# ScalarE zeroes the stacks, and TensorE transposes the identity between the foldings of the set-up

## The chip, the core and the metric

The kernel runs on one core of a Trainium2 chip. A core has a matrix engine (TensorE, PE in the profile, with its weight loads as PEld), a vector engine (VectorE, DVE), a scalar engine (ScalarE, ACT), a general engine (GpSimd, POOL) and an engine that here only issues transfers (SyncE, SP). The metric is the time of one execution on the device in microseconds; the lower, the better.

## What is computed

The reference applies two attention layers to x, which has 32 sequences of 256 tokens with 256 features. What matters of it here:

```python
# layer 0: linear attention, 8 heads of 32
xn = _ln(x, ln_w, ln_b)
q = softmax((xn @ Wq + bq).reshape(b, t, h, dh), axis=-1)
k = softmax((xn @ Wk + bk + (1.0 - src_mask) * -1000000.0).reshape(b, t, h, dh), axis=1)
v = ((xn @ Wv + bv) * src_mask).reshape(b, t, h, dh)
att = einsum('bnhd,bnhl->bhdl', k, v)
y = einsum('bnhd,bhdl->bnhl', q, att).reshape(b, t, d)
scale, shift = split(silu(emb) @ W_emb + b_emb)
x = x + silu(_ln(y, ln2_w, ln2_b) * (1 + scale) + shift) @ W_out + b_out
...
# layer 1: softmax attention, 16 heads of 16, then the same output block
att = softmax(einsum('bnhl,bmhl->bnmh', q, k) + (1.0 - mask) * -1000000.0, axis=2)
y = einsum('bnmh,bmhl->bnhl', att, v)
```

The weight and the bias of each first layer norm are constants of the inputs, so the kernel multiplies them into Wq, Wk and Wv once, before it uses these. This is the folding. A wide product is done as three products of float32r parts: each operand is split into a high part and the rest (a low part).

## The kernel before, in words

The program consists of one set-up (`prepared`) and of 32 sequences (`sequence(b)`), each with four parts a to d: layer 0 up to its values (a), the output block of layer 0 (b), the scores of layer 1 (c) and its output (d). Each step is an `Op` with an engine and a time. The times stand in two tables written out in the file: `SET_UP` for the set-up, and `STARTS` for a sequence, to which 26.2851 times the number of the sequence is added. `in_order` sorts all steps by these times and emits them; an engine executes its instructions in exactly that order. So a step that waits holds up everything that comes later on its engine. A list in `SET_UP` has one time for each use of a step's name, in the order in which the program creates them.

The set-up steps that matter here:

- `identity` (lines 264 to 267, GpSimd) makes the 128x128 identity `ident`. `identity_r` (269 to 275, VectorE) copies it to float32r and sums it to `fold` and `fold4`.
- `warmed` (277 to 280, TensorE) transposes the identity 16 times into a PSUM bank that nobody reads.
- `qk_zeros` (507 to 510, GpSimd) zeroes a stack: a pair of tiles, `qs` and `ks`, of 128 partitions by 2048 float32r each. There are three stacks (`ROOM["qk"]`), so there are six memsets. The times -674.55, -379.66 and -61.21 place two stacks at the head of GpSimd's queue and one after its first step of sequence 0. `qk_made` (512 to 515, SP) then writes a constant row into a stack.
- `w_high` (304) on ScalarE and `w_low` (307) on VectorE split a weight into its two parts (`parts`). The first of them is `wout0`: its `w_high` stands at -439.51, its `w_low` at -307.80.
- `w_rep` (316 to 323), `bias_scaled` (331) on VectorE, and `w_sums` (342 to 351) on TensorE, `w_scaled` (353) on VectorE are the folding of one weight. Per folding TensorE does two 6x256 matmuls (line 345) and four 128x256 matmuls in float32 (line 349). On VectorE the order is: `identity_r`, `token_terms`, the second `w_rep`, `w_low` of `wout0`, the first `w_rep`, `bias_scaled`. The first folding needs the last two.
- On TensorE the order is: `warmed`, `terms_turn` (449), the foldings of w02, w00 and w01, `e_product` (388), the turn of sequence 0 (565), the folding of w12, `e_sums` (399), the turn of sequence 1, and then the first products (558).
- In ScalarE's order, `split_high` of sequence 0 (752, at 4.18) comes directly before `k_kept` of sequence 1 (818, at -19.92 + 26.2851 = 6.37). `attention` (889, in the profile under 888) needs `k_kept`, and `k_sums` (895) and `blocks` (901) on VectorE need `attention`.

Of the kernel before, what the change touches and what calls it, by code (L numbers as in the profile page):

```python
# [10 lines left out]
F32 = mybir.dt.float32  # L11
# [5 lines left out]
P = 128  # L17
# [6 lines left out]
    bank=8, xt=9, nrm=4, x=4, h=2, g=6, k0=3, ek=1, mk=1, q0=1, y=2, eqT=2, v0=2, att=1, qkp=1, qk=3,  # L24
# [43 lines left out]
    identity_r=(-702.04,), load_bias=(-276.37,), load_bout=(-13.79, 53.66), load_cols=(-670.58,),  # L68
    load_cond=(-544.29,), load_emb=(-258.80, -217.52, -180.67, -207.44, -42.77, -14.95, -48.76, -2.89),
    load_masks=(-359.47,), load_w=(-291.77, -528.39, -390.22, -548.16, -39.72, -33.64, -88.51, -232.84),  # L70
    mask_terms=(-103.15,), p_made=(91.90, 5.63), qk_made=(-52.44, 60.07, 77.11), qk_zeros=(-61.21, -379.66,
    -674.55), qkp_made=(30.64,), terms0_store=(-141.84,), terms_rows=(-172.06,), terms_store=(-42.73,),
    terms_turn=(-333.70,), token_terms=(-574.41,), v0_made=(-369.51, -279.71), va_made=(-36.90, 52.97),
    w_high=(-50.10, -64.76, -198.98, -439.51, 25.73, 18.32, 14.13, -231.47), w_low=(-39.74, -58.97, -95.39,
    -307.80, 29.41, 24.14, 30.22, 4.56), w_rep=(-292.96, -366.10), w_scaled=(-76.66, -94.61, -210.46, 20.45,
    9.77, -47.81), w_sums=(-179.39, -114.53, -238.08, 19.55, 7.28, -54.52), warmed=(-409.56,),
    zero_one=(-762.96,), zero_one_store=(-98.07,),
)
LATE = dict(D=dict(late=2.2))
# [85 lines left out]
def tile_two_layers(ctx: ExitStack, tc: tile.TileContext, a: dict, out: bass.AP):  # L165
# [11 lines left out]
    nc = tc.nc  # L177
    x = a["x"]
    B, S, D = x.shape
# [7 lines left out]
    NSLOT = NU * NC  # L187
# [4 lines left out]
    const = ctx.enter_context(tc.tile_pool(name="const", bufs=1))  # L192
# [5 lines left out]
    def bank(dtype=F32):  # L198
        return psum.tile([P, 512], dtype, tag="bank", name="bank", bufs=ROOM["bank"])

    def f(ap):
        return ap.bitcast(F32)
# [5 lines left out]
    ident = const.tile([P, P], F32, name="ident")  # L208
    ident_r = const.tile([P, P], F32R, name="ident_r")
    fold = const.tile([P, B], F32, name="fold")  # L210
    one = const.tile([P, 1], F32, name="one")
    minus_half = const.tile([P, NBLOCK], F32, name="minus_half")
    fold4 = const.tile([P, P], F32, name="fold4")
    cols = const.tile([P, NCOL + 2 * NTOK], F32, name="cols")
# [26 lines left out]
    done = {}  # L241
# [11 lines left out]
    def prepared():  # L253
# [3 lines left out]
        def op(engine, time, run, *after, take=(), give=(), **more):  # L257
            ops.append(Op(engine, time, run, after, take, give, **(LATE.get(engine, {}) | more)))
            return ops[-1]
# [4 lines left out]
        def identity():  # L264
            make_identity(nc, ident)
            nc.gpsimd.memset(one, 1.0)
            nc.gpsimd.memset(minus_half, -0.5)

        def identity_r():
# [11 lines left out]

        o_cols = op("D", 0.3, load_cols)
        o = op("G", 0.9, identity)
        op("P", 0.11 * NWARM, warmed, o, take=("bank",), give=("bank",))
        done["ident"] = op("V", 0.13, identity_r, o)


# [152 lines left out]
        o = op("D", 0.3, load_bias)  # L440
# [17 lines left out]
        o = op("V", 0.2, token_terms, o_cols)  # L458
        o = op("P", 0.5, terms_turn, o, done["ident"], take=("bank",))
        o = op("V", 0.35, terms_rows, o, give=("bank",))  # L460
# [15 lines left out]
        o = op("D", 0.3, load_cond)  # L476
        o = op("A", 0.2, cond_tanh, o)
# [20 lines left out]
        o = op("D", 0.3, load_masks)  # L498
        o = op("V", 0.6, mask_terms, o)
# [7 lines left out]
        def qk_zeros():  # L507
            s.qk.append(qk_all.pop(0))
            for buf in s.qk[-1]:
                nc.gpsimd.memset(f(buf), 0.0)  # L510

        def qk_made():
            qk_bufs.append(s.qk.pop(0))
# [14 lines left out]
        o = op("G", 0.6, zero_one)  # L528
        o_stored = op("D", 0.3, zero_one_store, o)
        o_z = o_stored  # L530
        for n in range(ROOM["qk"]):
            o = op("G", 4.0, qk_zeros)
            o_z = op("D", 0.8, qk_made, o, o_z, give=("qk",))

        o_rep = norm_rows(1, o_cols)
# [630 lines left out]

    ctx.enter_context(tc.manual_schedule(engines=None))
    return in_order(prepared, [lambda b=b: sequence(b) for b in range(B)], ROOM)


# [67 lines left out]
```

## Time and profile before

| | |
|---|---|
| median of 3 runs | 918.5 us (918.21 to 922.14) |
| the profiled execution, own time | 914.85 us |
| its span | 912.7 us |
| TensorE busy | 864.9 us (95%) |
| VectorE busy | 813.5 us (89%) |
| ScalarE busy | 700.2 us (77%) |
| GpSimd busy | 692.4 us (76%) |
| mean granted clock of TensorE | 0.97 |

The span runs from the first to the last instruction on the core; the execution's own time is 2.15 us longer. A line of the timeline gives the start and the duration in microseconds, the engine, the line of the program, the instruction, what it writes from what, its shape, and in brackets how long the engine had been idle and what ended the wait. A line of the windows gives, for one stretch of time, the busy microseconds of each engine, the number of its instructions, and the TensorE clock granted (1.00 is full).

### The profile page before, as it was taken

The numbers are of one execution on the slowest core, as the hardware profiler recorded it, in microseconds if no ns is written. First come the engines' busy times: TensorE is split into PE (matmuls) and PEld (weight loads), VectorE is DVE, ScalarE is ACT, GpSimd is POOL, SyncE is SP. The second block draws the span as 40 slices with busy tenths as digits, with TensorE's granted clock in tenths as the row PEclk, the third lists the DMA queues.
The fourth block names the chain that finished last, engine by engine and source line by source line (L and its number), as shares of the span: only waits on it lengthen the run. The fifth ranks groups of instructions, "written<-read, shape, count | busy, mean of one in ns | idle before, by whom it ended". The sixth has DMA issues, their size and how long they took to land.

```text
span 912.7 us, 25210 instructions
## 1 busy us (share of the span) xinstructions
PE 864.9 (95%) x9494; PEld 705.0 (77%) x9494; DVE 813.5 (89%) x2235; ACT 700.2 (77%) x1420; POOL 692.4 (76%) x893
## 2 busy tenths in 40 slices
PE   6878899999999999999999999999999999999973
PEld 3667787888888888888888888888888888877642
DVE  6797989999999999999999999999999999999843
ACT  1365588788888898888888888888888888877762
POOL 5254567888888888988888888988888877775441
PEclk6799999999999999999999999999999999999985
DMA  6302222322232222223222212332233221222200
GB/s 215 108 16 88 84 81 81 102 104 97 103 103 74 89 71 90 102 104 103 96 104 86 86 60 92 104 102 104 96 104 103 71 82 57 87 86 86 95 14 24
DMA packets 56767, 81.09 MB, mean 89 GB/s; under 512 B 5407, under 2 KB 30021, under 8 KB 56646
## 3 DMA queue, kind: packets, MB, share of 16 engines
q1 hardware_dynamic: 56646, 79.47, 25.4%
q8 instruction: 76, 1.25, 0.6%
q14 instruction: 45, 0.37, 0.1%
HBM read 19.52 MB, written 8.55 MB: 31 GB/s over the span
## 4 chain that ended last, share of the span: by engine, by line
PE 79%; DVE 15%; POOL 2%; issue 1%; ACT 1%; DMA 0%; POOLq 0%; DVEq 0%; ACTq 0%
PE bank L558 37%; PE bank L1122 12%; PE bank L1100 9%; PE bank L1033 8%; PE bank L565 5%; DVE mx L1044 5%; PE bank L916 3%; PE bank L814 1%; PE bank L888 1%; DVE st L591 1%; PE bank L650 1%; PE bank L349 1%; DVE th L746 1%; DVE ident_r L270 1%; DVE yb L1138 1%
## 5 line engine op out<-in xcount | busy, mean ns | idle before, releaser
L1044 DVE TENSOR_REDUCE mx<-bank 128x2 f32<-128x512 f32 x512 | 324.9, 673 | 15.0 <-PE bank L1033 14.7
L1113 ACT ACTIVATE p<-bank 128x512 f32<-128x512 f32 x512 | 270.2, 600 | 84.1 <-PE bank L1100 78.5
L558 PE MATMUL bank<-xh,w_hi 128*128 128x256 f32 x512 | 153.1, 299 | 0.1
L558 PE MATMUL bank<-xl,w_hi 128*128 128x256 f32 x512 | 144.3, 282 | 1.2 <-DVE xl L707 1.2
L558 PE MATMUL bank<-xh,w_lo 128*128 128x256 f32 x512 | 143.9, 281 | 0.0
L1122 PE MATMUL bank<-p,va 128*32 128x256 f32 x2048 | 140.0, 386 | 0.1
L558 PE MATMUL bank<-wout_hi,hp 128*128 128x256 f32 x512 | 112.9, 302 | 10.0 <-ACT hp L752 9.5
L982 POOL TENSOR_TENSOR qk_lo<-nrm,qk_hi 128x512 fp32r<-128x512 f32 x58 | 74.7, 1287 | 56.5 <-ACT nrm L978 56.5
L1100 PE MATMUL bank<-qs,ks 64*128 64x256 f32 x1024 | 109.0, 311 | 4.3 <-DMA qs<-m_row 3.1
L1033 PE MATMUL bank<-ks,qs 64*128 64x256 f32 x1024 | 105.4, 307 | 1.0 <-DVE mx L1044 0.3
L1100 PEld LDWEIGHTS bank<-qs,ks 64*128 64x128 f32 x1024 | 73.8, 187 | 37.0 <-ACT p L1113 22.6
L558 PEld LDWEIGHTS bank<-xh,w_hi 128*128 128x128 f32 x512 | 97.1, 190 | 5.1 <-DVE mx L1044 0.4
L558 PEld LDWEIGHTS bank<-xl,w_hi 128*128 128x128 f32 x512 | 97.3, 190 | 1.6 <-DVE xl L707 1.6
L558 PEld LDWEIGHTS bank<-wout_hi,hp 128*128 128x128 f32 x512 | 86.3, 196 | 15.6 <-ACT hp L752 10.1
L1033 PEld LDWEIGHTS bank<-ks,qs 64*128 64x128 f32 x1024 | 73.6, 185 | 31.3 <-issue 13.4
L558 PEld LDWEIGHTS bank<-xh,w_lo 128*128 128x128 f32 x512 | 96.9, 189 | 0.0
L613 POOL TENSOR_SCALAR nrm<-xt,mv,off 128x256 f32<-128x256 f32 x116 | 65.0, 571 | 29.0 <-DVE off L608 26.1
L1122 PEld LDWEIGHTS bank<-p,va 128*32 128x32 f32 x2048 | 55.0, 109 | 41.1 <-ACT p L1113 1.8
L728 POOL TENSOR_TENSOR xt<-xt,bout 128x512 f32<-128x512 f32 x64 | 82.5, 1288 | 3.1 <-DMA bout<-in_bout_dram 3.1
L756 POOL TENSOR_TENSOR hp<-th,hp 128x512 fp32r<-128x512 f32 x58 | 74.9, 1292 | 9.1 <-ACT hp L752 9.1
L558 PE MATMUL bank<-w_hi,xh 128*128 128x256 f32 x256 | 78.2, 305 | 0.0
L707 POOL TENSOR_TENSOR xl<-nrm,xh 128x512 fp32r<-128x512 f32 x58 | 73.6, 1288 | 4.3 <-ACT nrm L703 4.3
(138 smaller groups left out, 2153.9 us busy)
## 6 DMA issues: line engine op xcount, KB each, us to landing
ks<-qk_hi SPq DMA_DIRECT2D x64, 256.0 KB
qs<-qk_hi SPq DMA_DIRECT2D x64, 256.0 KB
xt<-in_x_dram SPq DMA_DIRECT2D x32, 256.0 KB
ks<-qk_lo SPq DMA_DIRECT2D x32, 256.0 KB
qs<-qk_lo SPq DMA_DIRECT2D x32, 256.0 KB
out_dram<-xt SPq DMA_DIRECT2D x32, 256.0 KB
mk<-t_dram SPq DMA_DIRECT2D x32, 128.0 KB
raw<-in_w_dram SPq DMA_DIRECT2D x8, 256.0 KB
```

What stands on the lines that cost most here:

```text
L558: nc.tensor.matmul(o, left, right, start=(n == 0), stop=(n == len(pairs) - 1))
L565: nc.tensor.transpose(ps[:, ds(c * S + t * P, P)], src[:, t, ts(c, P)], ident)
L613: (nc.vector if s.quick else nc.gpsimd).tensor_scalar(s.nrm[:, t, :], get()[:, t, :], s.mv[:, t, 1:2], s.off[:, t : t + 1], ALU.mult, ALU.add)
L707: engine.tensor_tensor(s.xp[1], s.whole, f(s.xp[0]), ALU.subtract)
L728: nc.gpsimd.tensor_tensor(s.x, s.x, bout[:, i : i + 1, :].to_broadcast([P, NT, D]), ALU.add)
L756: engine.tensor_tensor(s.hp[1], s.th, f(s.hp[0]), ALU.subtract)
L982: engine.tensor_tensor(s.qkp[1][:, :, c], s.qk_ps[c], f(s.qkp[0][:, :, c]), ALU.subtract)
L1033: nc.tensor.matmul(ps[w][:, ts(m, S)], s.qs[half(w), u, c, ts(m, P)], s.ks[half(w), u, c, :], start=True, stop=True,)
L1044: nc.vector.tensor_reduce(s.mx[:, :, w, u, c], halves(s.s_ps[0, c, u][w]), AX.X, ALU.max, negate=True)
L1100: nc.tensor.matmul(ps[w][:, ts(m, S)], s.ks[half(w), u, c, ts(m, P)], s.qs[half(w), u, c, :], start=True, stop=True,)
L1113: nc.scalar.activation(s.pt[c, u][:, w], s.s_ps[1, c, u][w], AF.Exp)
L1122: nc.tensor.matmul(s.yT_ps[c][32 * j : 32 * j + 32, ts(v, S)], s.va[:, m, 8 * c + 4 * v + j, :], s.pt[c, 2 * v + j // 2][:, j % 2, ts(m, S ...
```

## The change

The six zeroing instructions leave GpSimd and become copies on ScalarE, whose source is a column of zeros (`nothing`) read 2048 times. The times of `qk_zeros` in the table change too: two stacks now stand at the head of ScalarE's queue (-650.21 and -640.66), and the third at 5.55, between `split_high` of sequence 0 and `k_kept` of sequence 1. TensorE gets four steps `heated`, each of six transposes of the identity into a bank that nobody reads. Their times put one after each of the foldings of w02, w00 and w01, and one after `e_product`. GpSimd gets one more small memset.

```diff
-    ... qk_zeros=(-61.21, -379.66, -674.55), ...
+    ... qk_zeros=(-650.21, -640.66, 5.55), ...
-    ... warmed=(-409.56,),
+    ... warmed=(-409.56,), heated=(-209.0, -146.0, -105.0, -80.0),
...
+    nothing = const.tile([P, 1], F32, name="nothing")
...
             nc.gpsimd.memset(one, 1.0)
+            nc.gpsimd.memset(nothing, 0.0)
             nc.gpsimd.memset(minus_half, -0.5)
...
         o = op("G", 0.9, identity)
+        done["zero"] = o
         op("P", 0.11 * NWARM, warmed, o, take=("bank",), give=("bank",))
+
+        def heated():
+            ps = bank()
+            for n in range(6):
+                nc.tensor.transpose(ps[:, ts(n % 4, P)], ident, ident)
+
+        for n in range(4):
+            op("P", 0.66, heated, o, take=("bank",), give=("bank",))
...
         def qk_zeros():
             s.qk.append(qk_all.pop(0))
             for buf in s.qk[-1]:
-                nc.gpsimd.memset(f(buf), 0.0)
+                nc.scalar.copy(buf.rearrange("p u c n -> p (u c n)"), nothing.to_broadcast([P, NSLOT * S]))
...
         for n in range(ROOM["qk"]):
-            o = op("G", 4.0, qk_zeros)
+            o = op("A", 4.0, qk_zeros, done["zero"])
             o_z = op("D", 0.8, qk_made, o, o_z, give=("qk",))
```

More of the change, by code (lines that the diff above doesn't have):

```diff
@@ L70 @@
     load_masks=(-359.47,), load_w=(-291.77, -528.39, -390.22, -548.16, -39.72, -33.64, -88.51, -232.84),
-    mask_terms=(-103.15,), p_made=(91.90, 5.63), qk_made=(-52.44, 60.07, 77.11), qk_zeros=(-61.21, -379.66,
-    -674.55), qkp_made=(30.64,), terms0_store=(-141.84,), terms_rows=(-172.06,), terms_store=(-42.73,),
+    mask_terms=(-103.15,), p_made=(91.90, 5.63), qk_made=(-52.44, 60.07, 77.11), qk_zeros=(-650.21, -640.66,
+    5.55), qkp_made=(30.64,), terms0_store=(-141.84,), terms_rows=(-172.06,), terms_store=(-42.73,),
     terms_turn=(-333.70,), token_terms=(-574.41,), v0_made=(-369.51, -279.71), va_made=(-36.90, 52.97),
@@ L75 @@
     -307.80, 29.41, 24.14, 30.22, 4.56), w_rep=(-292.96, -366.10), w_scaled=(-76.66, -94.61, -210.46, 20.45,
-    9.77, -47.81), w_sums=(-179.39, -114.53, -238.08, 19.55, 7.28, -54.52), warmed=(-409.56,),
+    9.77, -47.81), w_sums=(-179.39, -114.53, -238.08, 19.55, 7.28, -54.52), warmed=(-409.56,), heated=(-209.0, -146.0, -105.0, -80.0),
     zero_one=(-762.96,), zero_one_store=(-98.07,),
```

## The prediction

> **What bounds the kernel now.** I read the page first, then the windows of the fill and the drain, then the chain of waits and the timeline of the first 100 us.
>
> ```profile
> PEclk6799999999999999999999999999999999999985
> ...
> PE 79%; DVE 15%; POOL 2%; issue 1%; ACT 1%; DMA 0%; POOLq 0%; DVEq 0%; ACTq 0%
> ```
>
> From 100 us to 855 us TensorE has work almost all the time and makes up the chain. The change touches nothing there: it can only move the moment at which that stretch begins. So all is decided in the set-up, and a microsecond won or lost on its chain is one at the end, as the order of every engine is fixed. The first slices show a low clock, and the timeline shows why the set-up begins late:
>
> ```profile
> 1.80 1.82 POOL L510 MEMSET qs<- 128x2048 f32 x1
> 1.81 7.11 DVE L270 CAST ident_r<-ident 128x128 fp32r<-128x128 f32 x1 [0.29 <-POOL ident masks.py:199]
> ...
> 3.90 0.63 ACT L305 ACTIVATE wout_hi<-raw 128x512 fp32r<-128x512 f32 x1 [1.91 <-DMA raw<-in_w_dram]
> ...
> 7.02 1.82 POOL L510 MEMSET ks<- 128x2048 f32 x1
> ...
> 10.10 0.68 DVE L308 SCALAR_TENSOR_TENSOR wout_lo<-raw,wout_hi 128x512 fp32r<-128x512 f32 x1
> ...
> 11.70 1.21 PE L345 MATMUL bank<-bias,ident 6*128 6x256 f32 x2 [1.51 <-DVE bias L332]
> ```
>
> VectorE's small cast lasts 7.11 us, exactly as long as GpSimd's four memsets (1.80 to 8.84); a cast of half its partitions takes 0.24 us at 17.88. The memsets hold VectorE up. Behind the cast stand `wout_lo`, the first `w_rep`, the bias, and so TensorE's first folding at 11.70.
>
> The windows, each 3.41 us, show busy TensorE without clock:
>
> ```profile
> 1.55:4.97 3.42, 3.14 (x15) 3.14 (x16) 3.16 (x2) 1.27 (x3) 3.42 (x5) 1.00 0.82 209
> 4.97:8.38 3.41, 0.33 (x3) 0.09 (x1) 3.41 (x2) 0.00 (x0) 3.41 (x3) 1.00 0.84 301
> 11.79:15.21 3.42, 3.42 (x7) 1.94 (x8) 0.26 (x1) 0.63 (x1) 0.00 (x0) 0.50 0.82 267
> ...
> 28.86:32.27 3.41, 3.41 (x18) 3.41 (x18) 1.59 (x5) 1.27 (x2) 0.89 (x2) 0.50 0.48 126
> 32.27:35.68 3.41, 3.01 (x25) 2.81 (x24) 2.95 (x6) 0.00 (x0) 0.00 (x0) 1.00 0.76 225
> ```
>
> After the window, the first column is busy TensorE and the third from the end its clock. I chose these limits since the clock changes at 8.38, 32.25, 861.7, 865.1, 875.3, 882.1 and 892.4, and all distances are multiples of 3.41 us. From 11.7 to 32.25 the foldings run at half clock.
>
> **Part 1: two stacks at the head of ScalarE's queue.** GpSimd's four memsets go, and VectorE's cast ends at about 2.1 instead of 8.92. But VectorE executes in order, and its `wout_lo` needs ScalarE's `wout_hi`, which now stands behind four copies of 128x2048. No row shows such a copy. ScalarE's 128x128 activation takes 0.293 us, its 128x512 one 0.630, so 0.878 ns per element; its 128x512 casts in a row start 0.52 us apart. Estimate: 0.52 + 1536 x 0.878 ns = 1.87 us each, 7.5 us for four, hence from 1.9 to about 9.4. Then the table load (1.28 us in its row). It carries the line of `wout_hi`, the first ACTIVATE; the profile names copies COPY or CAST, so I take it to follow the four copies. Then `wout_hi` ends at 1.90 + 7.48 + 0.1 + 1.28 + 0.63 = 11.39, `wout_lo` begins at 11.43, and the folding, 1.60 us after it as before (10.10 to 11.70), at 13.03: **1.33 us later**. If the load still comes first, 11.74: 0.04 later. So the stall that goes is replaced by a wait for ScalarE. Nothing else gains: GpSimd's next work is at 17.58, and `cond_tanh` (4.44 before) is used at 16.08. SP's next weight load waits for `wout_lo` and slips with it; the last of the first four embedding weights is issued at 13.13 and used at 21.15.
>
> The page "ScalarE: Activation LUTs", section "What ACT_TABLE_LOAD costs", gives 186 ns + 0.833 ns per element, about 1.89 us for such a copy, and adds a drain of 1.38 us to the load. By that drain the folding would begin at 14.4; the trace has a load of 1.28 us and no such drain in view.
>
> **Part 2: the transposes.** In the trace 16 of them from 1.83 on start 0.213 us apart and last 421 ns; the last ones last 313 and 272, and 272 is what one lasts at full clock at 109 us. So transposes raise the clock: a window 92% full did it, and the idle one after it took it away at 8.38.
>
> The page "TensorE: Matmul & The Clock Gate", section "Part 4: PE-mode transpose", says that full clock doesn't engage for transposes. It speaks against this change: by it `heated` is pure cost, +5.1 us as in rival B. The durations above contradict it.
>
> Whether six are enough is open. Half clock: folding 3.15 us (11.70 to 14.85), `e_product` 1.87, turn 1.05, six transposes 6 x 0.213 = 1.28. Full clock: folding 0.62 + 1.07 = 1.69 (57.93 and 58.55), `e_product` 0.98 (43.92), turn 0.53, transposes 0.66 (four last 0.60 with their tail). Up to the end of sequence 0's turn: before 24.14 - 11.70 = 12.44; with the four groups 12.44 + 5.12 = 17.56 at half, 3 x 1.69 + 0.98 + 0.53 + 4 x 0.66 = 9.22 at full. If the clock comes g after the first folding's begin, 9.22 + 0.475 g, thus -3.2 + 0.475 g. After the turn, full clock brings VectorE's `eq` (32.45, 8.31 after the turn) forward to where VectorE's and ScalarE's own work puts it: activations 1.9, then a low part 0.7, `nrm` 0.8, `xl` 0.6, statistics 1.0, scaling 0.8, low part 0.7 = 6.5, so 1.8 sooner. In sum **-5.0 + 0.475 g**.
>
> A folding has 2.0 us of full-array matmuls and 1.15 us with six rows, which I count as nearly idle. Windows with up to about 62% such work kept half clock (892.4 to 895.9: ten matmuls of 0.213 us); those with about 84% or more raised it (878.7 to 882.1). A folding with a group lasts 4.43 us; a window of 3.41 us in it is filled 59% to 87%, depending on where it falls. With 70% as the point, about half of the positions rise in the first window (g about 4.6), a third in the second (9.3), the rest at 13.5. I take g = 6.8, **-1.8 us**; the ends are -3.4 (g = 3.4) and +5.1.
>
> **Part 3: the third stack at 51.8.**
>
> ```profile
> 51.20 0.62 ACT L752 CAST hp<-th 128x512 fp32r<-128x512 f32 x1
> 51.72 0.58 ACT L818 COPY kk<-bank 128x512 f32<-128x512 f32 x1
> ...
> 53.57 0.46 PE L888 MATMUL bank<-v,kk 128*32 128x33 f32 x32
> 53.95 0.70 DVE L873 STREAM_TRANSPOSE eqT<-eq 128x512 f32<-128x512 f32 x1
> 54.58 0.12 DVE L896 RECIPROCAL rk<-bank 128x2 f32<-128x2 f32 x1
> ```
>
> Two copies, 3.74 us, come between the first two rows. `kk` ends at 56.04 instead of 52.30. `attention` has 1.27 us to spare (52.30 to 53.57) and VectorE another 0.62 (54.03 to 54.65, when it is free for `rk`). The rest, 3.74 - 1.89 = **+1.85 us**, lands on the chain, which goes through `rk`, `att` and TensorE at 55.15. Queued behind on ScalarE are `xh` and `nrm` of sequence 3, two weight parts (used at 62.70) and `eq` (waits for GpSimd until 57.89); they can bear it. Ends: 0 if VectorE is late anyway, 3.74 if nothing is spare. The small memset costs 0.03.
>
> **Sum.** 1.33 - 1.8 + 1.85 = +1.4 us: 914.85 becomes 916.3 by the profiled execution. That execution lies 3.65 under the median of the runs shown; on the median the forecast is 919.9.
>
> **Rivals.**
> - A, the forecast: the clock comes in the first or second window. Between 1.85 + 0.04 - 2.8 and 1.85 + 1.33 - 0.6, so -0.9 to +2.6: 917.6 to 921.1. Chance 0.57.
> - B, the transposes cost and heat nothing: fp32 matmuls count for less than I assume, or windows fall badly, and no window before the turn reaches its point (between 62% and 84%). Price +5.1, in all 1.33 + 1.85 + 5.1 = +8.3 (+7.0 with the load first): 925.5 to 926.8, slower. For it: 20 us of busy TensorE got no clock. Against: only the filled share of those windows was low, at most about 60%. Chance 0.17.
> - C, cheap stacks: the table load first, the third stack hidden by a wait further on, and an early clock: 0.04 + 0 - 3.4 to 0, so 915.1 to 918.5. Chance 0.18.
> - D, ScalarE zeroes at half my price. The folding begins once its inputs are there, at about 9.1 (-2.6), the third stack is hidden, the clock gives -1.8 to -3.4: 912.5 to 914.1. The slope of two rows speaks against it. Chance 0.08.
> - The change doesn't do what it says: ScalarE's writes hold VectorE as GpSimd's do. The cast would then end at 9.4, `fold4` to the second `w_rep` (1.14 us) would follow while ScalarE loads its table, and the time is A's.
>
> **Numbers.** Half a per cent, 4.6 us, is about what a measurement of this kernel can tell from no change. Faster by more: D and the best of C, 0.10. Slower by more: B and the latest of A, 0.18. Within: 0.72. The range leaves out D and the last of B: 915.0 to 926.5.
>
> **What would show it.** On ScalarE four instructions of 1.8 to 2.0 us from 1.9 on, the table load behind them; VectorE's cast short, then idle until `wout_lo` at 11.4; TensorE's first folding at 13.0; the clock at 1.00 before 24 us and four groups whose transposes last 421 or 272 ns; `kk` 3.7 us after `hp`, `rk` about 1.9 us late. Wrong would be: the first folding before 11 (part 1), 0.50 up to 30 us (part 2), or `rk` following `eqT` at once (part 3).

## The result and the profile after

Twenty executions of the changed kernel have a median of 922.38 us (918.49 to 924.90), twenty of the kernel before 918.92 us (915.12 to 924.63). The ratio is 1.0037, with a 95% interval from 1.0023 to 1.0051: **slower by 0.37%**, some 3.4 us (3.5 between the medians). The forecast was 1.4 us slower, 919.9 us, with a range from 915.0 to 926.5.

The page of the changed kernel, the clock in 40 slices and the chain by engine:

```profile
span 920.0 us, 25253 instructions
PEclk8878999999999999999999999999999999999885
PE 80%; DVE 13%; ACT 3%; POOL 2%; issue 1%; DMA 1%; POOLq 0%; DVEq 0%; ACTq 0%
```

ScalarE has come onto the chain (3%, before 1%), VectorE has left part of it, and the clock in the first two slices is higher than before, that in the third and the fourth lower. The two profiled spans are 7.3 us apart, the medians only 3.5, so the comparison of the two profiles exaggerates; the size of an effect is taken below from the timed runs, its place from the profiles.

The begin, from the timeline (start, duration, engine, line, instruction):

```profile
0.71 1.28 ACT L521 ACT_TABLE_LOAD   x1 [0.71 <-PEq L1236]
1.81 0.23 DVE L272 CAST ident_r<-ident 128x128 fp32r<-128x128 f32 x1 [0.29 <-POOL ident masks.py:199]
2.01 1.90 ACT L521 CAST qs<-nothing 128x2048 fp32r<-128x2048 f32 x1
3.81 1.89 ACT L521 CAST ks<-nothing 128x2048 fp32r<-128x2048 f32 x1
...
9.21 0.63 ACT L316 ACTIVATE wout_hi<-raw 128x512 fp32r<-128x512 f32 x1
9.86 0.69 DVE L319 SCALAR_TENSOR_TENSOR wout_lo<-raw,wout_hi 128x512 fp32r<-128x512 f32 x1 [6.14 <-ACT wout_hi L316]
...
11.47 1.22 PE L356 MATMUL bank<-bias,ident 6*128 6x256 f32 x2 [5.56 <-DVE bias L343]
```

VectorE's cast lasts 0.23 us instead of 7.11: GpSimd's memsets had held it. VectorE then waits 6.14 us for `wout_hi`, which stands behind four copies, and the first folding begins at 11.47 instead of 11.70. A wait took the place of a stall.

The clock comes about 4.5 us after the first folding's begin. The first group of transposes still takes 1.49 us, and the matmuls behind it 0.73 instead of 1.22:

```profile
14.49 1.49 PE L292 MATMUL bank<-ident 128*128 128x128 f32 x6
15.91 0.73 PE L356 MATMUL bank<-bias,ident 6*128 6x256 f32 x2
```

The third stack, from the same timeline:

```profile
52.73 0.62 ACT L763 CAST hp<-th 128x512 fp32r<-128x512 f32 x1 [1.41 <-DVE th L757]
53.26 1.89 ACT L521 CAST qs<-nothing 128x2048 fp32r<-128x2048 f32 x1
55.06 1.89 ACT L521 CAST ks<-nothing 128x2048 fp32r<-128x2048 f32 x1
56.86 0.57 ACT L829 COPY kk<-bank 128x512 f32<-128x512 f32 x1
57.48 0.67 PE L899 MATMUL bank<-v,kk 128*32 128x33 f32 x32 [3.07 <-ACT kk L829]
58.22 0.17 DVE L907 RECIPROCAL rk<-bank 128x2 f32<-128x2 f32 x1 [2.91 <-PE bank L899]
58.42 0.62 DVE L912 SCALAR_TENSOR_TENSOR att<-bank,rk,diag 128x132 f32<-128x132 f32 x2
58.84 1.98 PE L927 MATMUL bank<-att,eqT 64*128 64x66 f32 x16 [0.69 <-DVE att L912]
```

Both brackets of waiting are new: TensorE waits 3.07 us for `kk`, VectorE 2.91 us for TensorE. From the end of `hp` to `att` it is now 5.07 us, before 2.92 (51.82 to 54.74): 2.15 more. And the sixteen matmuls of the last row take 1.98 us instead of 1.15, since the clock has gone meanwhile. Windows of the changed kernel (length, busy TensorE with its number of instructions, the granted clock, and at the end the share and the rate of the transfers):

```profile
43.35:46.76 3.41, 1.69 (x16) 1.00 0.00 0
53.59:57.00 3.41, 0.83 (x8) 1.00 0.00 0
57.40:60.80 3.40, 2.63 (x49) 0.50 0.00 0
```

At the end of the first window and of the second, in which TensorE is busy for half and for a quarter of the time, the clock falls to 0.50.

### The profile page after: what moved, and what is told of

Read it like the earlier page. It is cut to its first block, busy times and chain, and to the rows that moved or that the text cites. A ratio compares the mean times of both kernels' runs of the same rounds, so it can differ in the third digit from the quotient of the medians.

```text
span 920.0 us, 25253 instructions
## 1 busy us (share of the span) xinstructions
PE 870.0 (95%) x9518; PEld 714.2 (78%) x9518; DVE 809.5 (88%) x2235; ACT 710.4 (77%) x1426; POOL 680.3 (74%) x888
## 4 chain that ended last, share of the span: by engine, by line
PE 80%; DVE 13%; ACT 3%; POOL 2%; issue 1%; DMA 1%; POOLq 0%; DVEq 0%; ACTq 0%
PE bank L569 37%; PE bank L1133 12%; PE bank L1111 9%; PE bank L1044 8%; PE bank L576 5%; DVE mx L1055 4%; PE bank L927 3%; PE bank L825 1%; PE bank L899 1%; PE bank L661 1%; DVE st L602 1%; DVE th L757 1%; DVE yb L1149 1%; ACT qs L521 1%; ACT ks L521 1%
## 5 line engine op out<-in xcount | busy, mean ns | idle before, releaser
L569 PE MATMUL bank<-wout_hi,hp 128*128 128x256 f32 x512 | 114.5, 305 | 10.1 <-ACT hp L763 9.5
L569 PEld LDWEIGHTS bank<-wout_hi,hp 128*128 128x128 f32 x512 | 87.6, 198 | 15.8 <-ACT hp L763 10.1
```

Of the source, the lines that this page charges most:

```text
L569: nc.tensor.matmul(o, left, right, start=(n == 0), stop=(n == len(pairs) - 1))
```

## The experiments

One table first; each ratio is to the kernel before on the same chip, with its 95% interval.

| kernel | median, us | ratio |
|---|---|---|
| changed kernel | 922.38 | 1.0037 (1.0023 to 1.0051) |
| e1: without the groups of transposes | 922.27 | 1.0039 (1.0020 to 1.0059) |
| e2: before, with the groups alone | 918.84 | 1.0007 (0.9983 to 1.0031) |
| e3: changed, third stack earlier | 917.63 | 0.9980 (0.9958 to 1.0002) |
| e4: e3, with all copies behind `wout_hi` | 914.35 | 0.9960 (0.9936 to 0.9984) |
| e5: e4 without the groups | 915.01 | 0.9960 (0.9933 to 0.9987) |
| e6: before, with the third stack alone on ScalarE | 923.83 | 1.0050 (1.0028 to 1.0071) |
| e7: changed, the pause filled | 920.26 | 1.0011 (0.9989 to 1.0033) |
| e8: e4 with 40 transposes in `warmed` | 910.74 | 0.9907 (0.9870 to 0.9944) |
| e9: e8 without the groups | 912.64 | 0.9927 (0.9901 to 0.9953) |
| e10: before, with 64 transposes in `warmed` | 915.10 | 0.9961 (0.9941 to 0.9980) |

The theory after the result was that the third stack is the whole loss (its wait and the clock lost in it), that the transposes win a little, and that the first two stacks change nothing. The rival was that the transposes cost, or that the clock they win is lost again later.

**e1, the groups taken out.**

```diff
-        for n in range(4):
-            op("P", 0.66, heated, o, take=("bank",), give=("bank",))
```

> The changed kernel without its four groups of transposes; the zeroing on ScalarE stays. My theory: the third stack costs about 4 us (3.7 us of copies in front of kk, and a clock that drops in the pause), the transposes win about 2, the first two stacks change nothing. Then without the transposes the time is 1 to 3 us above the changed kernel, some 5 us above the kernel before; the first folding begins at 11.5 as after, the clock is 0.50 up to about 32 us. Rival, the transposes are what costs (24 more instructions, and a clock that is lost again at 26, 36 and 46 us because TensorE gets there too early): the time falls to within 1 us of the kernel before.

Measured 922.27 us, 0.1 under the changed kernel. Neither holds: the groups win nothing, and the loss stays without them.

**e2, the groups alone.** The kernel before with the lines of `heated` from the diff.

> The kernel before with the four groups of transposes alone; all zeroing stays on GpSimd. My theory: faster than the kernel before by 1 to 3 us, with full clock from the first or second folding on. Rival, the transposes cost: slower than the kernel before by 2 to 4 us, with clock losses between 26 and 60 us as in the changed kernel.

Measured 918.84 us, ratio 1.0007: level with the kernel before. A cost of 3.4 us is outside the interval, so the groups aren't what makes the changed kernel slower. A win of 1 us is inside it.

**e3, the third stack earlier.**

```diff
-qk_zeros=(-650.21, -640.66, 5.55)
+qk_zeros=(-650.21, -640.66, -150.0)
```

> The changed kernel with only the third stack's time moved, from 5.55 to -150: its two copies then stand behind the third folded weight part, at about 16.3 us, where ScalarE waits 6.7 us for TensorE. My theory: 3 to 5 us faster than the changed kernel, so level with the kernel before or up to 2 us under it; kk directly behind hp, and no clock loss at 57 us. Rival, the transposes cost: as the changed kernel within 1 us, since the pause at 57 us is only where the loss becomes visible.

Measured 917.63 us, 4.75 under the changed kernel, as the theory said. In the timeline of e3 the two copies stand where ScalarE waits anyway, and `kk` follows `hp` at once:

```profile
16.18 1.88 ACT L521 CAST qs<-nothing 128x2048 fp32r<-128x2048 f32 x1
17.96 1.89 ACT L521 CAST ks<-nothing 128x2048 fp32r<-128x2048 f32 x1
25.41 0.69 ACT L710 ACTIVATE xh<-bank,one 128x512 fp32r<-128x512 f32 x1 [5.55 <-PE bank L576]
```

```profile
50.24 0.62 ACT L763 CAST hp<-th 128x512 fp32r<-128x512 f32 x1
50.77 0.58 ACT L829 COPY kk<-bank 128x512 f32<-128x512 f32 x1
```

**e6, the third stack alone.** The kernel before, with the last stack's memsets as copies on ScalarE at 5.55; the other two stay on GpSimd.

```diff
+                if len(qk_all):
                     nc.gpsimd.memset(f(buf), 0.0)
+                else:
+                    nc.scalar.copy(buf.rearrange("p u c n -> p (u c n)"), nothing.to_broadcast([P, NSLOT * S]))
```

> The kernel before with one thing changed: the stack that was zeroed last goes to ScalarE at 5.55, between split_high and k_kept; the first two stay GpSimd's memsets, and there are no added transposes. My theory, that this stack is the whole loss: 3 to 4.5 us above the kernel before, with kk about 3.7 us after hp and a pause of TensorE of some 3 us before the attention of sequence 1. Rival, the loss needs the other stacks or the transposes too: within 1.5 us of the kernel before.

Measured 923.83 us, ratio 1.0050. This one move alone brings a loss as large as that of the whole change (the two intervals overlap). In the timeline TensorE has nothing from 53.6 to 58.19, and then runs at half clock:

```profile
58.19 0.67 PE L900 MATMUL bank<-v,kk 128*32 128x33 f32 x32 [4.59 <-ACT kk L830]
59.54 1.98 PE L928 MATMUL bank<-att,eqT 64*128 64x66 f32 x16 [0.68 <-DVE att L913]
```

**e7, the pause filled.** The changed kernel, with work for TensorE in the pause and no wait taken away. A time of 12.9 in the table puts the new step directly before `attention` of sequence 1.

```diff
+        def filled():
+            ps = bank()
+            for n in range(28):
+                nc.tensor.transpose(ps[:, ts(n % 4, P)], ident, ident)
+
+        op("P", 3.0, filled, o, take=("bank",), give=("bank",))
```

> The changed kernel with one more group of 28 transposes of the identity on TensorE, directly before the attention of sequence 1, so in the pause that the third stack makes (3 us at full clock). It removes no wait; it only keeps TensorE at work in it. If the clock lost in that pause costs 2 us beside the wait itself (1.9 us), the time falls 1 to 2.5 us below the changed kernel; if the wait is all, it stays within 0.7 us of it.

Measured 920.26 us, 2.1 under the changed kernel, with work added (the two intervals in the table overlap a little, so the 2.1 is rough). The clock keeps to 1.00 and the same sixteen matmuls take 1.11 us:

```profile
56.47 3.22 PE L301 MATMUL bank<-ident 128*128 128x128 f32 x28
59.62 0.46 PE L907 MATMUL bank<-v,kk 128*32 128x33 f32 x32
60.87 1.11 PE L935 MATMUL bank<-att,eqT 64*128 64x66 f32 x16 [0.79 <-DVE att L920]
```

So of the third stack's 4.75 us some 2.1 are the clock; the rest, 2.6, agrees with the 2.15 us by which `att` is later. (28 transposes are too many: `kk` is ready at 58.12 and the group ends at 59.69, so the clock may be worth more than the 2.1.)

The clock can be lost at this place without the third stack too, but for a shorter time. In the profiles of e2, e4, e5 and e8 it is gone for 3.4 us there (in e4 from 54.9 to 58.4), in those of before, e3 and e11 not at all. With the third stack it is gone for 6.8 us in the changed kernel, 10.3 in e1 and 13.7 in e6.

**e4, the copies behind `wout_hi`.**

```diff
-qk_zeros=(-650.21, -640.66, 5.55)
+qk_zeros=(-330.0, -329.0, -150.0)
```

> The changed kernel with all three stacks moved: the first two behind wout_hi and the tanh of the condition (-330 and -329 in the table), the third to -150. VectorE then waits neither for GpSimd nor for the copies. My theory, that the wait for ScalarE took the place of VectorE's stall in the first 11 us: the first folding begins at 7.5 to 9 us instead of 11.5, and the time is 2 to 4 us under the variant with only the third stack moved, 3 to 6 under the kernel before. Rival, the first folding waits for its inputs anyway or the start is given back to pauses without clock later: within 1 us of the variant with only the third stack moved.

Measured 914.35 us, 3.3 under e3. Now VectorE waits neither for GpSimd nor for the copies, as its timeline shows (0.86 us for `wout_hi` itself); the last thing to arrive is the bias, by a transfer:

```profile
4.59 0.69 DVE L319 SCALAR_TENSOR_TENSOR wout_lo<-raw,wout_hi 128x512 fp32r<-128x512 f32 x1 [0.86 <-ACT wout_hi L316]
...
7.72 0.28 DVE L343 TENSOR_SCALAR bias<-bias 6x256 f32<-6x256 f32 x1 [1.74 <-DMA bias<-in_bias_dram]
8.05 1.22 PE L356 MATMUL bank<-bias,ident 6*128 6x256 f32 x2 [2.12 <-DVE bias L343]
```

The first folding begins at 8.05, 3.4 us sooner than in e3 (11.48), and the medians differ by 3.3. That fits a gain that goes through to the end whole, but the two intervals overlap, and the two profiled executions don't show it: their spans are 914.8 us (e3) and 914.6 (e4). In them `q_exp`, the exponential of the queries, begins for sequence 0 and for sequence 5 as follows, e3 first and then e4:

```profile
34.81 0.63 ACT L880 ACTIVATE eq<-eq 128x512 f32<-128x512 f32 x1 [3.72 <-DVE eq L877]
120.94 0.63 ACT L880 ACTIVATE eq<-eq 128x512 f32<-128x512 f32 x1
```

```profile
31.22 0.63 ACT L880 ACTIVATE eq<-eq 128x512 f32<-128x512 f32 x1 [3.73 <-DVE eq L877]
120.83 0.63 ACT L880 ACTIVATE eq<-eq 128x512 f32<-128x512 f32 x1
```

Of a lead of 3.6 us 0.1 is left. In between, e4 loses its clock from 34.5 to 44.7 us and three times more before 86 us, e3 only from 79.2 to 86.1. So the lead can be given back before 100 us; that it comes out whole is not shown.

**e5, e4 without the groups** (the edit of e1).

> The variant whose copies stand behind wout_hi (stacks at -330, -329 and -150), without the four groups of transposes. It tells once more what these are worth where nothing else costs. If they win what they won up to the first turn in the changed kernel (1 to 2 us), the time is 1 to 2 us above the same variant with them, some 915.5; if their win is given back to clock losses between 26 and 90 us, within 1 us of it; if they cost, 1 to 3 us below it.

Measured 915.01 us, 0.66 above e4; the two intervals nearly coincide. It is the third pair (after and e1, e2 and before, e4 and e5) in which the groups win between -0.1 and 0.7 us; none of the three is told apart from 0.

**e8, TensorE kept busy up to the first folding.**

```diff
-NWARM = 16
+NWARM = 40
```

> The variant whose copies stand behind wout_hi, with 40 transposes in warmed instead of 16, so that TensorE works until the first folding at 8 us and the clock has no pause to be lost in. The first folding then lasts 1.7 us instead of 3.15, and the foldings end some 4 us sooner. If that reaches the end, 911 to 912.5; if it is given back in the losses of clock between 26 and 90 us, within 1 us of the same variant with 16 (914.4).

Measured 910.74 us: 3.6 under e4, and 0.93% under the kernel before (0.56% to 1.30%). It beats both kernels. Its six executions lie in two clusters, 907.0 to 908.2 us and 913.3 to 913.6, with the median between them, so the 3.6 is rough. Its timeline has every folding at full clock:

```profile
8.96 0.38 PE L460 MATMUL bank<-ident,tcol 128*32 128x128 f32 x2
9.27 0.69 PE L356 MATMUL bank<-bias,ident 6*128 6x256 f32 x2
9.89 1.13 PE L360 MATMUL bank<-raw,rep 128*128 128x256 f32 x4
10.86 0.82 PE L292 MATMUL bank<-ident 128*128 128x128 f32 x6
```

The first folding begins 1.2 us later than in e4, since the 40 transposes end at 9.1, and the turn of sequence 0 comes 3.2 us sooner (18.00 against 21.16). Of this lead 3.2 us are left at `q_exp` of sequence 5 (117.67 against 120.83).

**e9, e8 without the groups** (the edit of e1).

> The variant with 40 transposes in warmed and the copies behind wout_hi, without the four groups. If the clock, once granted, is kept by the foldings themselves, the foldings are 2.6 us shorter or as long as with the groups where TensorE waits anyway: 909 to 910.7. If the groups are needed to keep it, the clock is lost within the foldings and the time is 1 to 3 us above the 910.7 with them.

Measured 912.64 us, 1.9 above e8; the intervals overlap, so whether the groups help here stays open. In its profile the three foldings keep full clock without them, and the clock is lost at 20.0 us, after the folding of w12. The first part of the first expectation came true, its time did not: `e_product` takes 2.19 us instead of 1.07, as one of its weight loads waits 1.00 us for a transfer, and the folding of w12 waits 0.22 us for another. So here TensorE has caught up with the transfers of its weights.

**e10, the kernel before with a longer `warmed`.** One number, 64 instead of 16.

> The kernel before with one number changed: 64 transposes in warmed instead of 16. They last until about 10.5 us, so TensorE comes to the first folding at 11.7 at full clock. If the clock in the set-up is worth as much here as in the variant with 40 (3.6 us), 914.5 to 916; if it is not the clock but the earlier begin that told there, within 1 us of the kernel before.

Measured 915.10 us, ratio 0.9961 (0.9941 to 0.9980). So the longer `warmed` alone, with all zeroing left as it was, is worth 3.8 us (1.8 to 5.4). In its profile the first three foldings have full clock, but `q_exp` of sequence 0 begins only 1.65 us sooner than before (34.08 against 35.73); where the rest arises is not shown. One reason why it isn't more stands in the timeline: VectorE's two `nrm` instructions, beside GpSimd's memsets of the third stack (17.49 to 21.04), last 2.60 us instead of 0.73, and TensorE waits for them:

```profile
12.13 0.69 PE L345 MATMUL bank<-bias,ident 6*128 6x256 f32 x2
18.90 2.60 DVE L613 TENSOR_SCALAR nrm<-xt,mv,off 128x256 f32<-128x256 f32 x2
21.24 1.22 PE L565 MATMUL bank<-ident,nrm 128*128 128x128 f32 x4 [1.90 <-DVE nrm L613]
```

At 21.6 us the clock is lost.

**e11, the kernel before once more**, for a second profile.

> The kernel before, unchanged, for one more profile. Its first profile shows no loss of clock between 32 and 858 us and lies 3.7 us under the median of the runs shown. If losses of clock in the first 100 us are what tells a usual execution from that one, this profile shows some between 26 and 100 us, unless it happens to be as short as the first; if it shows none and lasts 918 us or more, the spread has another cause.

It took 914.91 us, as short as the first, and its profile differs from the first: the clock comes at about 23.4 us instead of 32.25, and is lost from 26.8 to 33.6, from 47.4 to 50.8 and from 81.4 to 84.8. Two different courses of the clock ended at the same time. What makes other executions of this kernel last up to 924 us stays open.

## Why the prediction was right, and where its sizes were off

**The side and the sum.** The forecast of +1.4 us was the sum of three terms, and none of the three had its size right. Measured: part 1 (two stacks at the head of ScalarE) 0.23 us sooner instead of 1.33 later; part 2 (transposes) 0 instead of -1.8; part 3 (third stack) +4.75 instead of +1.85. That the sum came within 2.5 us of the measured median is luck: the misses of +1.6, -1.8 and -2.9 us partly cancel. The measured 922.38 us lies in the range of none of the rivals, above A's 921.1 and below B's 925.5; only the wide stated range, which spans the gap between the two, holds it. The three measured sizes add up to 4.5 us and not to 3.4. e3, which has the change without the third stack's place, lies 1.2 us under the kernel before with an interval that touches 1, so the difference stays open.

Two slips in the prediction's figures: with its own shares for the three moments of the clock (a half, a third, the rest) the mean is 7.65 and not 6.8, hence -1.4 us instead of -1.8. And its chances for more than 4.6 us either way count C and A, which by their own ranges end at -3.4 and +2.6.

**Part 1: mechanism right, branch wrong.** The price of a copy was right (1.87 us expected; one lasts 1.89 and they start 1.80 apart), and so was that VectorE would wait for ScalarE. The step that failed is the choice that the table load would follow the copies: in the timeline it carries the line of the copy and lies at 0.71, before them. The prediction gave 11.74 for that case; it was 11.47. The drain of 1.38 us, which the page "ScalarE: Activation LUTs" of the Trainium skill adds to a load at a switch to another set (section "What ACT_TABLE_LOAD costs"), isn't to be seen at this first load: it ends at 1.99 and the first copy begins at 2.01.

**Part 2: mechanism right, base and mean wrong.** The 0 is rough: e2's interval reaches from -1.6 to +2.8 us. The transposes do raise the clock, against what the page "TensorE: Matmul & The Clock Gate" of the Trainium skill says of transposes in "Part 4: PE-mode transpose" (the profile lists the ones here as MATMUL): in e8, after 29 of them and nothing else, the last 11 take 1.36 us together, so they start 0.11 us apart, where the first ones are 0.213 us apart. The three moments foreseen, 4.6, 9.3 and 13.5 us after the first folding's begin, are those seen: about 4.5 in the changed kernel, 9.3 to 9.7 in e2, e3 and e4, 13.6 in e7. So the mean lies nearer to 9 than to the 6.8 taken. The second miss is the base. -5.0 + 0.475 g compares with an execution in which the clock came only at 32.25 us. Without groups it came at about 24.5 in e1 and 23.4 in e11 (by the durations of the instructions there) and at 27.2 in e5 (where the first folding had full clock as well, lost at 10.1). From the first folding's begin to the first `q_exp` of a profile it takes 22.2, 23.2, 23.3, 23.2 and 25.7 us with groups (after, e2, e3, e4, e7), in the mean 23.5; without them 24.0, 24.0, 23.0, 23.7 and 22.4 (before, e6, e1, e11, e5), in the mean 23.4. The groups pay for themselves and no more. Against the before's 24.03 the formula gives -0.6 for g = 9.2 and +1.5 for g = 13.6, and -0.8 and +1.7 were seen; for the changed kernel's own g = 4.5 it gives -2.9, and -1.8 was seen.

**Part 3: a term was missing.** The wait was expected at 1.85 and is 2.15 us. What the prediction left out is that TensorE, while it waits, loses its clock and then does `y_product` and what follows at half speed; e7 puts some 2.1 us on that. The prediction had the rule in hand, as it read the loss at 8.38 from a window that was nearly idle, but used it only for the set-up.

**The rivals.** B (the transposes cost and heat nothing) fell with e2; C (cheap stacks) and D (ScalarE at half the price) with the timeline, where the copies take 1.89 us and `kk` waits for them. That ScalarE's writes might hold VectorE fell too: `fold4`'s 128x128 instruction at 2.35, beside the first copy, takes 0.23 us, as it does at 8.96 in the kernel before.

**The premise.** That nothing changes between 100 us and the drain held: by the profiles the changed kernel is 6.50 us behind at `q_exp` of sequence 5 (126.01 against 119.51) and 6.80 at that of sequence 31 (791.14 against 784.34). That a microsecond of the set-up is one at the end did not hold in the profiles: e2, without the third stack on ScalarE, leads the kernel before by 0.8 us at `q_exp` of sequence 0 (34.92 against 35.73) and is 5.0 behind at that of sequence 5 (124.50 against 119.51), and e4 gives back its lead over e3. Before 100 us the clock still comes and goes, and the prediction has no term for that.

**Why the two profiles are 7.3 us apart** is only partly settled. From a lead of 2.07 us at `q_exp` of sequence 0 (33.66 against 35.73) it becomes a lag of 6.50 at that of sequence 5, so nearly all of it arises there. In the changed kernel's profile two small VectorE instructions beside GpSimd's wide ones took 1.34 and 1.31 us (48.55 and 49.82) instead of 0.24 and 0.18; in the profile before it was one, `wout_lo`, with 1.56 instead of 0.68. e7, with the same zeroing, has the short ones (and `wout_lo` with 1.21); e2 and e4 have such a pair of long ones (1.14 and 1.33, 1.15 and 1.33), e1 and e3 a long `wout_lo` (1.58 and 1.57). So which of the two an execution has doesn't follow the change. And the changed kernel's profile loses its clock six more times before 92 us, the profile before after 32.25 not once. How much such losses differ between executions of one kernel is to be seen in e11.

## What to carry to other kernels

Work moved to an idle engine is free only if nothing that comes later in that engine's order is awaited: look where the engine waits for something else (here at 16 us) and put it there, not merely where it has few instructions in all. A wait of a few microseconds on TensorE can cost twice, once as the wait and once as half speed behind it (e7), so price both. To have the clock at the begin of a chain, keep TensorE busy without a pause up to that begin (e8, e10), instead of paying for transposes inside the chain, which run at half clock until the grant comes and eat what they win (e2). And a lead won at the begin is sure only when the clock is steady behind it: compare the same step of several sequences in two profiles to see where a lead goes (e3 and e4).

## What the runs showed of the hardware that was not expected

- The profile's clock column shows 1.00 up to its first recorded change, also where the instructions run at half clock: in e1 it says 1.00 from the start to 28 us, while the foldings take 1.22 and 2.08 us, as at 0.50. Durations of one known instruction (a transpose: 421 or 272 ns) are the better witness.
- The clock isn't only lost to idleness: a window of 3.41 us with TensorE busy for 1.69 us lost it (43.35 to 46.76). In the kernel before, 1.99 us in a window from 35.68 to 39.10 kept it.
- ScalarE's copies of 128x2048 did nothing to VectorE's small instructions (a 128x128 one takes 0.23 us beside them), where GpSimd's memsets of the same tiles held a 128x128 cast for 7.11 us, and two `nrm` in e10 for 2.60.
